# A four-layer graph network on one core: later hand-offs between engines in layers L2 and L3, and a node's own row loaded from the table

## The chip, the core and the metric

The kernel runs on one core of a Trainium2 chip. The metric is the device time of one execution in microseconds (us); the time of a kernel is the median over its runs. The core's engines run side by side, each taking its own instructions in order: PE (TensorE, matrix products), DVE (VectorE, elementwise), ACT (ScalarE, functions and copies), POOL (GpSimd, which here issues the indirect gathers) and SP (SyncE, which issues plain transfers). They wait for each other on semaphores.

## The reference, cut to what matters

There are 6250 nodes with 256 features and 100000 edges sorted by destination node. Four layers follow each other; each takes `h = relu(layernorm(x))` and adds its result to `x`. The change touches the last two:

```python
# L2: attention over a node's incoming edges
h = x @ Wn.T + bn
e = edge_attr @ We.T + be
a = leaky_relu(sum((h[src] + e) * attn, axis=-1), 0.01)
a = exp(a - m[dst]);  a = a / (segment_sum(a, dst)[dst] + 1e-16)
x = x + relu(segment_sum(h[src] * a, dst))
# L3: graph convolution with a self loop
norm = dinv[src] * dinv[dst]           # dinv = 1/sqrt(degree + 1)
x = x + relu(segment_sum((x' @ W)[src] * norm, dst) + b)   # x' = relu(layernorm(x)), src and dst with loops
```

So for each edge a row of a table of nodes has to be fetched by the number in `src`, weighted, and summed at the number in `dst`.

## The kernel before

Nodes are cut into 49 blocks of 128 (`NB`), edges into 98 groups (`G`) of 8 x 128 (`J` = 8 columns of `P` = 128 edges). One layer writes the table that the next one gathers from: L1 writes `xt2` (258 numbers a row) by blocks, L2 gathers from it and writes `xt3` (256 numbers a row), L3 gathers from that and writes the output. A gather (line 130, an indirect DMA that POOL issues) fetches 128 rows by 128 indices, so a group takes 8 of them and a layer 784. All of a layer's gathers depend on the whole table before them.

What is done for a group `g`: DVE makes a one-hot matrix `oh` for each of the 8 columns (line 1095 in L2, with the edge's weight `ex` in it, which ACT makes by an exponential on line 1092; line 1150 in L3, from the destination alone). PE multiplies it with the gathered rows `vg` and sums the 8 products in PSUM (`sum_tiles`, line 681; an f32 product shows as two instructions, so a group is 16). ACT copies the sum to SBUF (`ws`, line 691 in L2, 1175 in L3). Consecutive groups cover overlapping windows of 128 nodes, 64 apart, so when all groups of a block are summed, `sum_block` (line 699) puts three or four windows together with shift matrices on PE: 6 or 8 instructions. `blocks_done(g)` names the block whose last group is `g`: every second group ends one block, and the last group, 97, ends block 48 (block 47 ends with group 96).

What is done for a finished block in L2: `out2` divides by the sum of weights, applies relu (ACT, line 1106), adds to `x`, and makes the layer norm: statistics on DVE (145, 146), a square root on ACT (126), `xn` on DVE (1110). Then `turned2` transposes on PE (1116) with a relu on ACT (1118), and `table3_row` multiplies with `L3_gnn_W` on PE (1124), scales on ACT (1125) into `rows3`, a part of the large tile `big`, and SP writes the block of `xt3` (1126). In L3, `end3` adds the node's own row from `rows3`, scales, adds the bias, applies relu and adds `x` (DVE, 1156, 1157, 1159), and SP writes the output (1161).

The order of the work in both layers is written out by hand under `manual_schedule`: each engine gets its instructions in the order in which the program's loop over `g` names them. In step `g` of L2 the order is: gathers of group `g`; `sum_block` of the block that ended with `g-1`; `turned2` of the one that ended with `g-2`; `one_hot2(g)`; `out2` of the `g-1` block; the group's sum and its copy; `table3_row` of the `g-2` block. In L3: gathers of `g`; `sum_block` of the `g-1` block; the sum of `g`; `one_hot3(g+1)`; the copy; `end3` of the `g-1` block.

Gathered rows lie in 5 buffers in L2 (4 groups are issued before the check `bound2`, whose result decides a branch on line 1078 that is not taken with these inputs) and in 6 buffers in L3. A gather waits until its buffer is free.

Of the kernel before, what the change touches and what calls it, by code (L numbers as in the profile page):

```python
# [10 lines left out]
F32 = mybir.dt.float32  # L11
I32 = mybir.dt.int32
AF = mybir.ActivationFunctionType
OP = mybir.AluOpType
# [3 lines left out]
P = 128  # L18
J = 8
W = 128  # L20
D = 256
# [14 lines left out]
def tile_gnn(ctx: ExitStack, tc: tile.TileContext, a: dict, out: bass.AP, N: int):  # L36
# [287 lines left out]
    def make_windows(ps, pool, win, relw=None):  # L324
# [7 lines left out]
        for i, op in enumerate((OP.min, OP.max)):  # L332
            nc.vector.tensor_reduce(lohi[:, i, :], dstf, AX.X, op)
            t = ps("A", [P, P])
            nc.tensor.transpose(t[:G, :], lohi[:, i, :], ident)
            nc.vector.tensor_reduce(ends[:, i:i + 1], t[:G, :], AX.X, op)
            t = ps("B", [P, P])
            nc.tensor.transpose(t[:, :G], ends[:, i:i + 1].to_broadcast([G, P]), ident[:G, :G])
            nc.vector.tensor_copy(ends_b[:, i, :], t[:, :G])
# [316 lines left out]
    def fast():  # L656
# [406 lines left out]
        ps = fctx.enter_context(Psum("ps2", S=2, A=1, T=2, B=2, C=1))  # L1063
        w3 = weights(wp, "L3_gnn_W", D, D)
        brow = on_all(wp, "L3_gnn_b", D)
        bufs2, ahead = 5, 4
        with tc.tile_pool(name="e2", bufs=2) as ep:
            vgs, gots, sums, normed = {}, {}, {}, {}

            def rows2(g):  # L1070
                vgs[g] = ep.tile([P, J, TR], F32, name="vg", bufs=bufs2)
                gots[g] = [gather(vgs[g][:, j, :], xt2, src_i[:, g * J:(g + 1) * J], j) for j in range(J)]
# [11 lines left out]
            def one_hot2(g):  # L1084

                gs = slice(g * J, (g + 1) * J)
                al = ep.tile([P, J], F32, name="al")
                nc.vector.tensor_tensor(al[:, :, None], vgs[g][:, :, D:D + 1], te[:, gs][:, :, None], OP.add)  # L1088
                leaky(al, al, 0.01)
                nc.vector.tensor_tensor(al, al, shift[:, gs], OP.subtract)  # L1090
                ex = ep.tile([P, J], F32, name="ex")
                nc.scalar.activation(ex, al, AF.Exp)  # L1092
                oh = ep.tile([P, J, P], F32, name="oh")
                for j in range(J):
                    made_g = nc.vector.tensor_scalar(oh[:, j, :], iota, rel[:, g * J + j:g * J + j + 1],  # L1095
                                                     ex[:, j:j + 1], OP.is_equal, OP.mult)
                return oh, made_g

            def out2(b, s):
# [9 lines left out]
                xn = ep.tile([P, D], F32, name="xn", bufs=1)  # L1109
# [3 lines left out]
            def turned2(xn):  # L1113
                t = ps("B", [P, 2, P])
                for k in range(2):
                    nc.tensor.transpose(t[:, k, :], xn[:, k * P:(k + 1) * P], ident)
                hb = ep.tile([P, 2, P], F32, name="hb")
                nc.scalar.activation(hb, t, AF.Relu)
                return hb

            def table3_row(b, hb):
# [3 lines left out]
                nc.scalar.activation(rows3[:, b, :], t, AF.Copy, scale=dinv[:, b:b + 1])  # L1125
                nc.sync.dma_start(xt3[b * P:(b + 1) * P, :], rows3[:, b, :])

            with tc.manual_schedule():
                for g in range(G + 2):
                    if ahead <= g < G:  # L1130
                        rows2(g)
                    summed = [(b, sum_block(sums, b, TR)) for b in blocks_done(g - 1)]
                    turned = [(b, turned2(normed[b])) for b in blocks_done(g - 2)]
                    if g < G:
                        oh, made_g = one_hot2(g)
                    for b, s in summed:
                        normed[b] = out2(b, s)
                    if g < G:
                        sums[g], _ = sum_window(ep, oh, vgs[g], TR, made_g, gots[g])
                    for b, hb in turned:  # L1140
                        table3_row(b, hb)


        with tc.tile_pool(name="e3", bufs=2) as ep, tc.manual_schedule():
            sums = {}

            def one_hot3(g):
                oh = ep.tile([P, J, P], F32, name="oh")
# [3 lines left out]
                return oh, made_g  # L1152

            def end3(b, s):
                r0, r1 = b * P, min(N, (b + 1) * P)
                nc.vector.tensor_tensor(s, s, rows3[:, b, :], OP.add)  # L1156
# [6 lines left out]
            oh, made_g = one_hot3(0)  # L1163
            for g in range(G + 1):
                if g < G:
                    vg = ep.tile([P, J, D], F32, name="vg", bufs=6)
                    got = [gather(vg[:, j, :], xt3, src_i[:, g * J:(g + 1) * J], j) for j in range(J)]
                summed = [(b, sum_block(sums, b, D)) for b in blocks_done(g - 1)]
                if g < G:
                    s = ps("S", [P, D])  # L1170
                    sum_tiles(s, [(oh[:, j, :], vg[:, j, :]) for j in range(J)], made_g, got)
                    if g + 1 < G:
                        oh, made_g = one_hot3(g + 1)
                    sums[g] = ep.tile([P, D], F32, name="ws", bufs=6)
                    nc.scalar.activation(sums[g], s, AF.Copy)
                for b, s in summed:
                    end3(b, s)
# [343 lines left out]
```

## Time and profile before

| | us |
|---|---|
| median of 6 runs | 4505.54 (4501.85 to 4507.66) |
| the profiled execution, device time | 4501.38 |
| its span, first to last instruction | 4499.6 |
| granted TensorE clock, mean share of full speed | 0.823 |

| part of the span | from, us | to, us | what is there |
|---|---|---|---|
| L2, gathers | 2497.8 | 3483.2 | 784 gathers, first start to last end |
| between | 3483.2 | 3502.0 | no gather |
| L3, gathers | 3502.0 | 4484.8 | 784 gathers |
| end | 4484.8 | 4499.6 | no gather |

Layers L0 and L1 and the part between L1 and L2 take the first 2497.8 us; the program that the change touches runs after them. Times of lines are from the span's start. A line of a timeline reads: start, duration, engine, line, operation, output and inputs with shapes, how many instructions are merged, and in brackets how long the engine was idle before and what ended the wait. The L-numbers of lines (L130) are lines of the kernel, not layers.

### The profile page before, as it was taken

The page shows a single profiled execution, that of the slowest core. Times are in us where ns is not written, and L with a number is a line of the kernel's source. Part 1 is how long each engine was busy: PE and PEld are TensorE (multiplying, and loading weights), DVE is VectorE, ACT ScalarE, POOL GpSimd, SP SyncE. Part 2 cuts the span into 40 slices and gives each one's busy share as a digit, 9 for nine tenths or more (in the row PEclk, how much of TensorE's full clock was granted, in tenths as well). Part 3 has the DMA queues.
Part 4 walks back from the last instruction along what each step waited for, and adds up shares of the span by engine and source line. Part 5 has one row for each costly group of instructions (what it writes and reads, how often), then busy time and mean ns, then how long its engine had stood idle before and what let it go on. Part 6 is the DMA issues. An engine that isn't in the chain of part 4 may idle for free. (4 is left out here: it accounts for less than half of the span.)

```text
span 4499.6 us, 42030 instructions
## 1 busy us (share of the span) xinstructions
PE 3068.7 (68%) x12132; PEld 2381.2 (53%) x12133; DVE 2101.7 (47%) x6391; ACT 619.7 (14%) x1559; POOL 3057.8 (68%) x3215
## 2 busy tenths in 40 slices
PE   7788888888897666666556566666566556666656
PEld 4377777776645444444445345445455444444444
DVE  5476655665524566766667333333333222222222
ACT  3211010000124100000000122222222000000000
POOL 0377777777501677777777677777777677777776
PEclk9888888888898777777887688888888788788888
DMA  3355555555500344444444344444443333333333
GB/s 105 113 180 168 162 159 161 161 163 161 155 1 14 110 128 125 123 125 123 129 126 115 88 112 113 111 113 113 112 113 110 97 112 111 112 112 111 112 112 101
DMA packets 258740, 536.78 MB, mean 119 GB/s; under 512 B 65096, under 2 KB 144966, under 8 KB 258502
## 3 DMA queue, kind: packets, MB, share of 16 engines
q0 software_dynamic: 137984, 364.28, 28.5%
q1 hardware_dynamic: 107750, 156.85, 11.3%
q10 hardware_dynamic: 12768, 12.85, 0.9%
q8 instruction: 105, 1.72, 0.2%
q14 instruction: 133, 1.09, 0.1%
HBM read 504.57 MB, written 29.15 MB: 119 GB/s over the span
## 5 line engine op out<-in xcount | busy, mean ns | idle before, releaser
L130 POOL DMA_INDIRECT vg<-xt,src_i x1568 | 1488.4, 949 | 519.1 <-issue 486.4
L681 PE MATMUL ps_S<-vg,oh 128*128 128x258 f32 (+1 forms) x3136 | 992.0, 485 | 775.6 <-DMA vg<-xt,src_i 409.2
L681 PEld LDWEIGHTS ps_S<-vg,oh 128*128 128x128 f32 x3136 | 765.1, 250 | 994.3 <-issue 386.8
L130 POOL DMA_INDIRECT xbuf<-vt,src_i x784 | 783.0, 999 | 241.1 <-issue 211.0
L130 POOL DMA_INDIRECT big<-ht,src_i x784 | 743.5, 948 | 246.3 <-issue 181.1
L681 PE MATMUL ps_S<-oh,big 128*128 128x128 f32 x1568 | 310.6, 379 | 338.1 <-DVE big L1026 296.5
L1150 DVE TENSOR_SCALAR oh<-iota,rel 128x128 f32<-128x128 f32 x784 | 166.8, 302 | 740.9 <-PE ps_S L681 738.7
L681 PE MATMUL ps_S<-xbuf,oh 128*128 128x265 f32 x1568 | 487.1, 476 | 12.9 <-issue 11.6
L681 PEld LDWEIGHTS ps_S<-oh,big 128*128 128x128 f32 x1568 | 288.4, 284 | 368.6 <-DVE big L1026 247.5
L681 PEld LDWEIGHTS ps_S<-xbuf,oh 128*128 128x128 f32 x1568 | 368.0, 241 | 99.2 <-issue 16.3
L763 PE MATMUL ps_A<-scw,to 128*128 128x16 f32 x1568 | 224.3, 287 | 114.5 <-DVE to L748 114.5
L763 PEld LDWEIGHTS ps_A<-scw,to 128*128 128x128 f32 x1568 | 220.7, 224 | 133.8 <-issue 85.6
L1095 DVE TENSOR_SCALAR oh<-iota,rel,ex 128x128 f32<-128x128 f32 x784 | 214.5, 369 | 145.6 <-ACT ex L1092 145.6
L699 PE MATMUL ps_T<-ws,shifts 128*128 128x265 f32 (+2 forms) x1164 | 278.7, 382 | 0.0
L691 ACT ACTIVATE ws<-ps_S 128x265 f32<-128x265 f32 (+1 forms) x196 | 76.3, 389 | 1226.1 <-PE ps_S L681 1226.1
L1026 DVE TENSOR_TENSOR big<-big,ps_A 128x384 f32<-128x384 f32 (+1 forms) x294 | 132.3, 505 | 230.4 <-DMA big<-ht,src_i 225.6
L699 PEld LDWEIGHTS ps_T<-ws,shifts 128*128 128x128 f32 x1164 | 220.8, 190 | 33.7
L836 DVE TENSOR_TENSOR xbuf<-xbuf,ps_E 128x2048 f32<-128x2048 f32 x98 | 223.6, 2282 | 21.5 <-ACT ps_E L774 21.5
L980 PE MATMUL ps_A<-wr,rb 99*128 99x384 f32 (+1 forms) x588 | 214.0, 504 | 9.4 <-DMA rb<-in_rbf 9.4
L1088 DVE TENSOR_TENSOR al<-vg,te 128x8 f32<-128x8 f32 x98 | 16.4, 168 | 426.1 <-DMA vg<-xt,src_i 426.1
L988 DVE TENSOR_SCALAR oh<-iota,rel,cut 128x128 f32<-128x128 f32 x784 | 211.3, 361 | 0.0
L900 POOL TENSOR_TENSOR xbuf<-xbuf,bout 128x1024 f32<-128x1024 f32 (+1 forms) x13 | 29.0, 2228 | 256.5 <-ACT xn L898 249.6
(226 smaller groups left out, 3043.7 us busy)
## 6 DMA issues: line engine op xcount, KB each, us to landing
drow<-in_dst_row SPq DMA_DIRECT2D x98, 512.0 KB
ea<-in_edge_attr SPq DMA_DIRECT2D x98, 512.0 KB
vg<-xt,src_i POOLq DMA_INDIRECT x1568
xbuf<-vt,src_i POOLq DMA_INDIRECT x784
big<-ht,src_i POOLq DMA_INDIRECT x784
rb<-in_rbf SPq DMA_DIRECT2D x196, 49.5 KB
vt<-row SPq DMA_DIRECT2D x49, 132.5 KB
xt<-row SPq DMA_DIRECT2D x49, 129.0 KB
```

What stands on the lines that cost most here:

```text
L130: return nc.gpsimd.indirect_dma_start(out=rows, out_offset=None, in_=table, in_offset=bass.IndirectOffsetOnAxis(ap=idx[:, j:j + 1], axis=0))
L681: m = wait_for(nc.tensor.matmul(s, l, r, start=j == 0, stop=j == len(pairs) - 1), made)
L691: nc.scalar.activation(ws, s, AF.Copy)
L699: nc.tensor.matmul(t, shift_by(s), sums[g], start=i == 0, stop=i == len(parts) - 1)
L763: nc.tensor.matmul(dgs[g][:, j, :], tos[g][:, j * P:(j + 1) * P], scw[:, g // 2, g % 2, :], start=True, stop=True)
L836: made_g = nc.vector.tensor_tensor(vals, vals, ex[:, :, :, None].to_broadcast([P, J, H, HD]), OP.mult)
L900: nc.gpsimd.tensor_tensor(x[:, b0:b1, :], x[:, b0:b1, :], w1["bout"][:, None, :].to_broadcast([P, b1 - b0, D]), OP.add)
L980: filtered[g] = nc.tensor.matmul(t, rbs[g][0:33 * n, g % 2, q, :], wr3[0:33 * n, 0:n, :], start=True, stop=True)
L988: nc.vector.tensor_scalar(ohs[g][:, j, :], iota, rel[:, c], w1["cut"][:, c], OP.is_equal, OP.mult)
L1026: made_g = nc.vector.tensor_tensor(hg[:, js, :], hg[:, js, :], t, OP.mult)
L1095: made_g = nc.vector.tensor_scalar(oh[:, j, :], iota, rel[:, g * J + j:g * J + j + 1], ex[:, j:j + 1], OP.is_equal, OP.mult)
L1150: made_g = nc.vector.tensor_scalar(oh[:, j, :], iota, rel[:, g * J + j:g * J + j + 1], None, OP.is_equal)
```

## The change

In L2 and L3, whatever one engine makes for another is used at least one step of a group later than it is made, as written in the loop:

- L2: `one_hot2(g+1)` is made in step `g` (before, `one_hot2(g)`). The sum's copy (`taken`) is made one step after the sum. `sum_block` comes at 2 steps after the block's last group, `out2` at 3, `turned2` at 4, its relu `hb` at 5, `table3_row` at 6, the scaled row and its write (`row3`) at 7. Before they came at 1, 1, 2, 2, 2 and 2. The loop has 105 steps where it had 100.
- L2: gathered rows lie in six views of `big`, used in the order 3, 4, 5, 0, 1, 2; a gather waits by hand for the end of the sum that used the view six groups earlier. Three groups are gathered before the check, where it was four. PSUM has three slots for sums (it had two), and the tag `A` is gone.
- L3: one-hots are made two steps ahead, the copy is made one step after the sum, `sum_block` comes 2 steps and `end3` 3 steps after the block's last group (before: 1 and 1). PSUM is given out anew: four slots for sums, three for blocks. Rows lie in six views of `big`.
- As `big` now holds gathered rows, `rows3` is gone from both layers: L2 puts a scaled row into one of three small tiles and writes it to `xt3`, and L3 loads a block's own 128 rows back from `xt3` by one SP transfer (`own`) at the step of the block's last group.
- In `make_windows`, which runs only behind branches that are not taken with these inputs, a PSUM tag is `B` where it was `A` (left out below).

```diff
@@ -1060,16 +1060,24 @@
 
 
 
-        ps = fctx.enter_context(Psum("ps2", S=2, A=1, T=2, B=2, C=1))
+
+        psc2 = fctx.enter_context(ExitStack())
+        ps = psc2.enter_context(Psum("ps2", S=3, T=2, B=2, C=1))
         w3 = weights(wp, "L3_gnn_W", D, D)
         brow = on_all(wp, "L3_gnn_b", D)
-        bufs2, ahead = 5, 4
+
+        ahead = 3
         with tc.tile_pool(name="e2", bufs=2) as ep:
-            vgs, gots, sums, normed = {}, {}, {}, {}
+            vgs, gots, ohs, wins, ends, sums, blocks, normed = {}, {}, {}, {}, {}, {}, {}, {}
+            views = []
+            views += [big[:, i * J * TR:(i + 1) * J * TR].rearrange("p (j t) -> p j t", j=J) for i in (3, 4, 5, 0, 1, 2)]
 
             def rows2(g):
-                vgs[g] = ep.tile([P, J, TR], F32, name="vg", bufs=bufs2)
-                gots[g] = [gather(vgs[g][:, j, :], xt2, src_i[:, g * J:(g + 1) * J], j) for j in range(J)]
+                i = g % len(views)
+                vgs[g] = views[i]
+                gots[g] = [wait_for(gather(vgs[g][:, j, :], xt2, src_i[:, g * J:(g + 1) * J], j),
+                                    *([ends[g - len(views)]] if g >= len(views) else []))
+                           for j in range(J)]
 
             with tc.manual_schedule():
                 for g in range(ahead):
@@ -1083,6 +1091,8 @@
 
             def one_hot2(g):
 
+                if g >= G:
+                    return
                 gs = slice(g * J, (g + 1) * J)
                 al = ep.tile([P, J], F32, name="al")
                 nc.vector.tensor_tensor(al[:, :, None], vgs[g][:, :, D:D + 1], te[:, gs][:, :, None], OP.add)
@@ -1090,11 +1100,25 @@
                 nc.vector.tensor_tensor(al, al, shift[:, gs], OP.subtract)
                 ex = ep.tile([P, J], F32, name="ex")
                 nc.scalar.activation(ex, al, AF.Exp)
-                oh = ep.tile([P, J, P], F32, name="oh")
+                oh = ep.tile([P, J, P], F32, name="oh", bufs=4)
                 for j in range(J):
                     made_g = nc.vector.tensor_scalar(oh[:, j, :], iota, rel[:, g * J + j:g * J + j + 1],
                                                      ex[:, j:j + 1], OP.is_equal, OP.mult)
-                return oh, made_g
+                ohs[g] = oh, made_g
+
+            def summed(g, n):
+
+                if g < G:
+                    wins[g] = ps("S", [P, n])
+                    oh, made_g = ohs.pop(g)
+                    ends[g] = sum_tiles(wins[g], [(oh[:, j, :], vgs[g][:, j, :]) for j in range(J)],
+                                        made_g, gots[g])
+
+            def taken(ep, g, n):
+
+                if 0 <= g < G:
+                    sums[g] = ep.tile([P, n], F32, name="ws", bufs=8)
+                    nc.scalar.activation(sums[g], wins.pop(g), AF.Copy)
 
             def out2(b, s):
 
@@ -1106,7 +1130,7 @@
                 nc.scalar.activation(s[:, 0:D], s[:, 0:D], AF.Relu, scale=rd)
                 nc.vector.tensor_tensor(x[:, b, :], x[:, b, :], s[:, 0:D], OP.add)
                 norm_stats(b, b + 1)
-                xn = ep.tile([P, D], F32, name="xn", bufs=1)
+                xn = ep.tile([P, D], F32, name="xn", bufs=2)
                 nc.vector.tensor_scalar(xn, x[:, b, :], mv[:, b, 0:1], rstd[:, b, :], OP.subtract, OP.mult)
                 return xn
 
@@ -1114,67 +1138,90 @@
                 t = ps("B", [P, 2, P])
                 for k in range(2):
                     nc.tensor.transpose(t[:, k, :], xn[:, k * P:(k + 1) * P], ident)
-                hb = ep.tile([P, 2, P], F32, name="hb")
-                nc.scalar.activation(hb, t, AF.Relu)
-                return hb
+                return t
 
             def table3_row(b, hb):
                 t = ps("C", [P, D])
                 for k in range(2):
                     nc.tensor.matmul(t, hb[:, k, :], w3[:, k, :], start=k == 0, stop=k == 1)
-                nc.scalar.activation(rows3[:, b, :], t, AF.Copy, scale=dinv[:, b:b + 1])
-                nc.sync.dma_start(xt3[b * P:(b + 1) * P, :], rows3[:, b, :])
-
+                return t
+
+            def row3(b, t):
+                row = ep.tile([P, D], F32, name="row3", bufs=3)
+                nc.scalar.activation(row, t, AF.Copy, scale=dinv[:, b:b + 1])
+                nc.sync.dma_start(xt3[b * P:(b + 1) * P, :], row)
+
+            turns, hbs, cs = {}, {}, {}
             with tc.manual_schedule():
-                for g in range(G + 2):
-                    if ahead <= g < G:
-                        rows2(g)
-                    summed = [(b, sum_block(sums, b, TR)) for b in blocks_done(g - 1)]
-                    turned = [(b, turned2(normed[b])) for b in blocks_done(g - 2)]
-                    if g < G:
-                        oh, made_g = one_hot2(g)
-                    for b, s in summed:
-                        normed[b] = out2(b, s)
-                    if g < G:
-                        sums[g], _ = sum_window(ep, oh, vgs[g], TR, made_g, gots[g])
-                    for b, hb in turned:
-                        table3_row(b, hb)
-
-
+                one_hot2(0)
+                for g in range(G + 7):
+                    if ahead <= g + 1 < G:
+                        rows2(g + 1)
+                    for b in blocks_done(g - 2):
+                        blocks[b] = sum_block(sums, b, TR)
+                    for b in blocks_done(g - 4):
+                        turns[b] = turned2(normed.pop(b))
+                    for b in blocks_done(g - 6):
+                        cs[b] = table3_row(b, hbs.pop(b))
+                    one_hot2(g + 1)
+                    for b in blocks_done(g - 3):
+                        normed[b] = out2(b, blocks.pop(b))
+                    summed(g, TR)
+                    taken(ep, g - 1, TR)
+                    for b in blocks_done(g - 5):
+                        hbs[b] = ep.tile([P, 2, P], F32, name="hb")
+                        nc.scalar.activation(hbs[b], turns.pop(b), AF.Relu)
+                    for b in blocks_done(g - 7):
+                        row3(b, cs.pop(b))
+
+
+        psc2.close()
+        ps = fctx.enter_context(Psum("ps3", S=4, T=3))
         with tc.tile_pool(name="e3", bufs=2) as ep, tc.manual_schedule():
-            sums = {}
+            sums, blocks, ohs, wins, vgs, gots, ends, owns = {}, {}, {}, {}, {}, {}, {}, {}
+            views = []
+            views += [big[:, i * J * D:(i + 1) * J * D].rearrange("p (j t) -> p j t", j=J)
+                      for i in range(2 * NACC // (J * D))]
 
             def one_hot3(g):
-                oh = ep.tile([P, J, P], F32, name="oh")
+                if g >= G:
+                    return
+                oh = ep.tile([P, J, P], F32, name="oh", bufs=4)
                 for j in range(J):
                     made_g = nc.vector.tensor_scalar(oh[:, j, :], iota, rel[:, g * J + j:g * J + j + 1], None,
                                                      OP.is_equal)
-                return oh, made_g
+                ohs[g] = oh, made_g
+
+            def rows3_(g):
+                if g < G:
+                    vgs[g] = views[g % len(views)]
+                    gots[g] = [wait_for(gather(vgs[g][:, j, :], xt3, src_i[:, g * J:(g + 1) * J], j),
+                                        *([ends[g - len(views)]] if g >= len(views) else []))
+                               for j in range(J)]
 
             def end3(b, s):
                 r0, r1 = b * P, min(N, (b + 1) * P)
-                nc.vector.tensor_tensor(s, s, rows3[:, b, :], OP.add)
+                nc.vector.tensor_tensor(s, s, owns[b], OP.add)
                 nc.vector.scalar_tensor_tensor(s, s, dinv[:, b:b + 1], brow, op0=OP.mult, op1=OP.add)
                 y = ep.tile([P, D], F32, name="y3")
                 nc.vector.scalar_tensor_tensor(y, s, 0.0, x[:, b, :], op0=OP.max, op1=OP.add)
                 if r1 > r0:
                     nc.sync.dma_start(out[r0:r1, :], y[0:r1 - r0, :])
 
-            oh, made_g = one_hot3(0)
-            for g in range(G + 1):
-                if g < G:
-                    vg = ep.tile([P, J, D], F32, name="vg", bufs=6)
-                    got = [gather(vg[:, j, :], xt3, src_i[:, g * J:(g + 1) * J], j) for j in range(J)]
-                summed = [(b, sum_block(sums, b, D)) for b in blocks_done(g - 1)]
-                if g < G:
-                    s = ps("S", [P, D])
-                    sum_tiles(s, [(oh[:, j, :], vg[:, j, :]) for j in range(J)], made_g, got)
-                    if g + 1 < G:
-                        oh, made_g = one_hot3(g + 1)
-                    sums[g] = ep.tile([P, D], F32, name="ws", bufs=6)
-                    nc.scalar.activation(sums[g], s, AF.Copy)
-                for b, s in summed:
-                    end3(b, s)
+            one_hot3(0)
+            one_hot3(1)
+            for g in range(G + 3):
+                rows3_(g)
+                for b in blocks_done(g):
+                    owns[b] = ep.tile([P, D], F32, name="own", bufs=3)
+                    nc.sync.dma_start(owns[b], xt3[b * P:(b + 1) * P, :])
+                for b in blocks_done(g - 2):
+                    blocks[b] = sum_block(sums, b, D)
+                summed(g, D)
+                one_hot3(g + 2)
+                taken(ep, g - 1, D)
+                for b in blocks_done(g - 3):
+                    end3(b, blocks.pop(b))
 
 
     def slow():
```

More of the change, by code (lines that the diff above doesn't have):

```diff
@@ L333, in make_windows @@
             nc.vector.tensor_reduce(lohi[:, i, :], dstf, AX.X, op)
-            t = ps("A", [P, P])
+            t = ps("B", [P, P])
             nc.tensor.transpose(t[:G, :], lohi[:, i, :], ident)
```

## The prediction

> **What bounds the kernel now.** I read the busy time by stage first, then the waits of POOL, then the two stretches in which POOL is idle, line by line. Busy time in five stretches (us; columns PE, PEld, DVE, ACT, POOL, then the granted TensorE clock):
>
> ```profile
> 2497.80:3483.20 985.40, 608.23 (x2202) 485.30 (x2202) 350.09 (x1406) 243.44 (x475) 744.07 (x784) 0.83 0.40 112
> 3483.20:3502.00 18.80, 12.14 (x54) 9.21 (x52) 9.47 (x41) 5.61 (x13) 0.00 (x0) 0.94 0.10 30
> 3502.00:4484.80 982.80, 589.27 (x1934) 464.96 (x1934) 226.23 (x910) 37.16 (x97) 744.30 (x784) 0.80 0.38 111
> 4484.80:4499.60 14.80, 5.27 (x24) 4.08 (x22) 2.70 (x6) 0.38 (x1) 0.02 (x1) 0.89 0.10 31
> ```
>
> L2 and L3 each take 784 gathers. POOL is busy 744 of some 984 us, but its gaps are not waits. Its waits from 2497 us on (total us, times, longest):
>
> ```profile
> POOL vg L130 <- issue: 486.4, 1531, 20.4
> POOL vg L130 <- DMA xt<-big: 18.9, 1, 18.9
> POOL vg L130 <- DMA vg<-xt,src_i: 3.7, 3, 3.1
> ```
>
> 1531 gaps wait for nothing that the profile shows: they are 0.30 us each, one behind every gather, except for the 20.4 us before L2's first. Gather (0.95) and gap (0.30) make a start-to-start time of 1.25 us, and 783 x 1.25 = 979 us of L2's 984.4 and L3's 981.9 us from first to last start. What is left over is 3.1 us at one gather in L2 (the thirty-third, behind the branch on line 1078), and some 2.4 and 2.7 us by which gathers beside DVE's work are longer than 0.95 (1.01 to 1.04 us beside the one-hots of 4002, 4010 and 4021 us). So POOL's issue rate sets both layers, and apart from it there are only the two stretches without gathers, in which a chain runs: the last gather lands, the rest of the layer is made, and its result is written.
>
> **The steady part: what the change can gain there.** PE waits 349.6 us for `oh` of line 1095 and DVE 738.7 us for PE's sums before line 1150; these are waits of engines with room, and the later hand-offs may remove all of them without starting one gather earlier. What could be gained is the 3.1 us and the 5.1 us of longer gathers. The first stays: at the branch POOL waits for the landing of the gather before it (2536.64 to 2540.67), now the 24th and not the 32nd; the flag it tests was made at 2500.3 and DVE passed the branch at 2510.4, long before 24 x 1.25 = 30 us have passed since 2497.8. The second stays too, as the same one-hots are made at the same pace; its ends are 0 and twice the 5.1 us.
>
> The Trainium skill, "Perfetto Trace Analysis", section "Optimization Strategies", says to keep the matmul engine as busy as one can and to speed up whatever it waits for. By it the 349.6 us that PE waits for one-hots would be the size of the gain, a time near 4156 us. This trace disagrees: 1531 gaps of POOL wait for no engine at all.
>
> Does a new wait reach POOL? A view comes free at the end of the sum six groups before. In groups of 10.02 us, group g-6 starts 60 us ahead of group g; it takes 10 us to issue, 2 to land, up to 10 for the step that the sum now lies behind and up to 6.7 for the sum. That leaves over 30 us: no cost, and three views fewer would be needed before POOL stops. `own` (49 transfers of 128 KB on SP) is issued with its block's last group, 30 us before `end3`; a write of that size took 2.6 us from its scaled row to the next gather (3499.35 to 3502.01): no cost (uncovered, it would be 2.6 us once, at the end), and SP's later output write stands behind it by one issue of 0.33 us. Dropping `rows3` costs ACT and SP the same instructions as before.
>
> **The first drain, L2 to L3.** Now (start, duration, idle before):
>
> ```profile
> 3485.59 0.17 DVE L1090 TENSOR_TENSOR al<-al,shift 128x8 f32<-128x8 f32 x1
> 3486.03 0.20 ACT L1092 ACTIVATE ex<-al 128x8 f32<-128x8 f32 x1
> 3486.27 2.14 DVE L1095 TENSOR_SCALAR oh<-iota,rel,ex 128x128 f32<-128x128 f32 x8 [0.51 <-ACT ex L1092]
> 3488.46 3.75 PE L681 MATMUL ps_S<-vg,oh 128*128 128x258 f32 x16 [1.10 <-DVE oh L1095]
> 3493.56 0.16 DVE L1104 TENSOR_SCALAR rd<-ps_T 128x1 f32<-128x1 f32 x1 [2.09 <-PE ps_T L699]
> 3498.88 0.47 ACT L1125 ACTIVATE big<-ps_C,dinv 128x256 f32<-128x256 f32 x1 [1.22 <-PE ps_C L1124]
> ```
>
> When the last gather lands (3485.2), block 47 has already been summed (1.90 us, at 3485.46); its `out2` runs beside the last sum, and only block 48 follows. By the new lags block 46 is at `out2`, block 47 not yet summed, and the order on each engine is fixed. Three things come into the chain:
> - An exponential behind a square root needs a table load. Before, `ex` of group 97 followed that of 96 with no square root between; now `out2` of block 45 lies between `ex` of 96 and of 97. Such a load is seen at 3475.76: 1.28 us, begun when `al` was there, with `ex` right behind. By those rows `oh` would start at 3487.37, 1.10 later. The sum ends at 3493.31.
> - PE sums block 47 next: 1.90 us by the row of 3485.46, so DVE starts its `out2` at about 3495.1.
> - `out2` of 47, from `rd` to the end of `xn`, is a chain between DVE and ACT that took 3.12 us for block 48 (3493.56 to 3496.68). Block 48's can begin only behind it on DVE: 3498.2, where it began at 3493.56. Its own sum is done by then.
>
> That is 4.7 us; behind it the chain is the one of before. With the free-running overlap between engines and `table3_row` of 47 ahead of 48's (1.0 us, partly beside the transposes' relu) my bounds are 4.0 and 5.5. Rows of blocks 46, 47 and 48 are written within 3 us, where it was two: 0 to 0.5, I take 0.2.
>
> The Trainium skill, "ScalarE: Activation LUTs", section "What ACT_TABLE_LOAD costs", adds a drain of about 1.38 us to a load of 1.28. By it the whole change would cost 1.4 us more. In this trace `ex` starts 0.02 us behind the load (3477.06), so I leave the drain out.
>
> **The second drain, the end.** PE now, from the last two groups on:
>
> ```profile
> 4476.77 6.58 PE L681 MATMUL ps_S<-vg,oh 128*128 128x256 f32 x16 [6.35 <-DMA vg<-xt,src_i]
> 4483.19 1.89 PE L699 MATMUL ps_T<-ws,shifts 128*128 128x256 f32 x8
> 4486.99 3.69 PE L681 MATMUL ps_S<-vg,oh 128*128 128x256 f32 x16 [1.91 <-DMA vg<-xt,src_i]
> 4490.52 1.46 PE L699 MATMUL ps_T<-ws,shifts 128*128 128x256 f32 x6
> ```
>
> Two things change. First, block 47's sum, which ran at 4483.19 while group 97 was landing, falls behind the last sum, and its `end3` (4492.01 to 4493.44, so 1.43) ahead of block 48's: 1.89 + 2 x 1.43 less what 48 had to wait anyway (4490.68 to 4493.44, 2.76) is 2.0 us. Second, the last sum loses what kept the clock up. Group 96's sum, after 6.35 us idle, had a granted clock of 0.54 and took 6.58; group 97's, after 1.91 us idle, had 1.00 and took 3.69. In L3 the even groups' sums took 5.2 to 6.7 us, with a median of 6.0. With `sum_block` now a step later it follows the odd groups' sums, not the even ones', and the last group finds PE idle since some 5 us. I take 6.0, so 2.3 us more; ends 0 (it stays at 3.69) and 3.0. Sum of the second drain: 4.3 us. In the first drain the last sum follows group 96's closely, so it stays at full clock.
>
> **The sum.** 4.7 + 0.2 + 2.0 + 2.3 = 9.2 us. On the profiled execution's 4501.38 that is 4510.6; the median of before lies 4.2 above that execution, so against it I predict 4514.7, +0.20%. The line between no change and slower is 0.2%, 9.0 us, about what a measurement of this kernel can tell from no change; the forecast lies just over it.
>
> **The rivals.**
> - The other side, not slower: the last L3 sum stays warm. It decides alone: from 0.2 us less than my 6.0 us on, the total is under 9.0 us; at 3.69 it is 6.9 us, 4512.4. For it: odd sums of 3.69 exist, and 5 us idle is less than the 6.35 of the slow ones. Against it: early in L3 odd sums after about 5 us idle took 5.2. Chance 0.31.
> - The change doesn't do what it says at the tails: engines don't keep the loop's order. For it: `al` of group 0 ran at 2509.82, ahead of DVE's branch that stands before it. If block 47 is summed ahead of the last sum in both layers, 1.9 + 3.1 and 2.0 go: 2.2 us, 4507.7. Chance 0.10.
> - Contention: one-hots made earlier fall beside other gathers. If every group of L3 had one gather of 1.03 and not 0.95, 98 x 0.08 = 7.8 us: 17.0 us, 4522.5. Against it: one-hots still start when a sum frees their slot. Chance 0.10.
> - Faster: the drains cost nothing and both the 3.1 and 5.1 us go: 4497.3, which isn't even 0.2%. Chance 0.04, for what I don't see.
>
> **How the numbers follow.** The forecast, 9.0 to about 13 us, has 0.45; with contention slower has 0.55. The warm sum and the kept order make 0.41 for no change. The range: drains at 4.0 + 0 + 2.0 + 0 less 3 of the 5.1 us is 3.0; drains at 5.5 + 0.5 + 2.0 + 3.0 and 4 us of the contention is 15: 4508.5 to 4520.5. By its own bounds alone the likeliest case has 4514.6 to 4518.5.
>
> **What would show it.** Right: the start-to-start time of gathers stays at 1.25 us in both layers; PE's and DVE's waits shrink; the gap without gathers between L2 and L3 grows from 18.9 to about 23.7 us, with a table load before the last `ex`, and line 699 for block 47 behind the last sum in both layers; the end from the last gather grows from 14.8 to about 19.1. Wrong: gathers that wait for PE, DVE or an earlier landing more than once, or a gap between layers no longer than before.

## The result, and the profile after

The changed kernel takes 4514.08 us (median of 17 runs, 4509.93 to 4518.18) where the kernel before takes 4502.94 (37 runs, the six shown at first among them). The ratio is 1.0025 with a 95% interval of 1.0018 to 1.0031, so 8 to 14 us slower. Predicted were 4514.7 and slower; the time lies in the range. That the change costs time is clear; the line of 0.2% that the prediction drew lies within the interval, so on which side of that line the loss falls is not decided. The reasons were right in kind and place. But of the four terms of the sum, the first drain and the slow last sum were too small, the rest of the end was too large, and the third write of a row did not show; and two costs in L2, an instruction of POOL's at the branch and longer gathers, were not in the sum at all.

In seven of the twelve experiments every kernel, the one before too, had a median of 5210 to 5260 us, and in their traces PE starts its instructions slowly; these seven stand last, each beside the kernel before on the same chip.

Busy time by stage of the profiled execution (span 4513.9 us, 14.3 over before; columns as before: PE, PEld, DVE, ACT, POOL, granted clock):

```profile
2474.20:2495.40 21.20, 11.59 (x36) 7.04 (x35) 12.10 (x32) 1.98 (x8) 0.95 (x1) 0.61 0.08 23
2495.40:3485.00 989.60, 612.07 (x2184) 482.16 (x2184) 349.00 (x1399) 226.74 (x465) 746.26 (x784) 0.81 0.40 111
3485.00:3511.90 26.90, 18.81 (x71) 14.15 (x69) 8.91 (x36) 9.18 (x21) 0.06 (x2) 0.82 0.10 32
3511.90:4494.90 983.00, 590.80 (x1926) 465.04 (x1926) 229.04 (x923) 37.16 (x97) 744.49 (x784) 0.79 0.40 118
4494.90:4513.90 19.00, 9.76 (x30) 7.77 (x30) 2.60 (x6) 0.38 (x1) 0.00 (x0) 0.68 0.08 24
```

Of the 14.3 us, L2's gathers take 4.2 (985.4 to 989.6), the stretch between the layers 8.0 (POOL's idle time, 18.86 to 26.84; the rows are cut at tenths), L3's gathers 0.2, the end 4.2 (14.8 to 19.0); the time up to L2's first gather is 2.3 shorter, in a part that the change leaves alone. POOL's waits (total us, times, longest):

```profile
POOL big L130 <- issue: 458.7, 1506, 0.3
POOL big L130 <- DMA xt<-row: 26.8, 1, 26.8
POOL big L130 <- DVE oh L1105: 5.1, 1, 5.1
```

As before, almost every gap is the 0.30 us that waits for nothing. Gathers still start every 1.25 us: no new wait reached POOL in the steady part. What grew is the wait for the table's last rows and the one gap behind the branch, which was 3.1 us (the 5.1 us that the profile puts down to DVE's one-hot). In L2 the gathers themselves grew too, from 949 to 952 ns on average.

The chain in the first drain, from the last landing on (start, duration, idle before):

```profile
3487.49 0.17 DVE L1100 TENSOR_TENSOR al<-al,shift 128x8 f32<-128x8 f32 x1
3487.74 1.28 ACT L1102 ACT_TABLE_LOAD   x1 [4.38 <-DVE al L1100]
3489.28 2.14 DVE L1105 TENSOR_SCALAR oh<-iota,rel,ex 128x128 f32<-128x128 f32 x8 [1.62 <-ACT ex L1102]
3491.47 5.44 PE L681 MATMUL ps_S<-big,oh 128*128 128x258 f32 x16 [1.85 <-DVE oh L1105]
3496.75 1.90 PE L699 MATMUL ps_T<-ws,shifts 128*128 128x258 f32 x8
3498.69 0.16 DVE L1128 TENSOR_SCALAR rd<-ps_T 128x1 f32<-128x1 f32 x1 [4.21 <-PE ps_T L699]
3501.61 0.15 DVE L1128 TENSOR_SCALAR rd<-ps_T 128x1 f32<-128x1 f32 x1
3506.59 2.08 PE L1146 MATMUL ps_C<-l_gnn_w,hb 128*128 128x256 f32 x4 [0.56 <-ACT row L1151]
3508.76 0.47 ACT L1151 ACTIVATE row<-ps_C,dinv 128x256 f32<-128x256 f32 x1 [2.22 <-PE ps_C L1146]
```

Everything that the prediction put into this chain is there: the table load, block 47's sum behind the last group's, its `out2` (3498.69) ahead of block 48's (3501.61). Two things are there that it didn't have: the last sum takes 5.44 us where it took 3.75, and block 48's product waits 0.56 us for the scaling of block 47's row and then takes 2.08 us where it took 1.13. That product ran at half the clock, and so did nearly all of the last sum of L3 (granted clock third from the end):

```profile
4497.00:4503.60 6.60, 6.60 (x17) 5.29 (x18) 0.00 (x0) 0.00 (x0) 0.00 (x0) 0.53 0.00 0
3506.60:3508.70 2.10, 2.07 (x4) 1.17 (x4) 0.00 (x0) 0.00 (x0) 0.00 (x0) 0.50 0.18 62
```

PE at the end:

```profile
4486.92 3.69 PE L681 MATMUL ps_S<-big,oh 128*128 128x256 f32 x16 [1.75 <-DMA big<-xt,src_i]
4497.00 6.74 PE L681 MATMUL ps_S<-big,oh 128*128 128x256 f32 x16 [6.39 <-DMA big<-xt,src_i]
4503.57 3.18 PE L699 MATMUL ps_T<-ws,shifts 128*128 128x256 f32 x14
```

The parity has turned round, as said: group 96's sum is now the fast one, the last group's is slow after 6.39 us idle, and both blocks' sums (14 instructions) stand behind it.

### The profile page after: what moved, and what is told of

Same layout as the page of the kernel before. It is cut to its first block, busy times and chain, and to the rows that moved or that the text cites. A ratio compares the mean times of both kernels' runs of the same rounds, so it can differ in the third digit from the quotient of the medians.

```text
span 4513.9 us, 42171 instructions
## 1 busy us (share of the span) xinstructions
PE 3083.2 (68%) x12132; PEld 2388.7 (53%) x12133; DVE 2103.5 (47%) x6391; ACT 606.0 (13%) x1557; POOL 3059.4 (68%) x3215
## 3 DMA queue, kind: packets, MB, share of 16 engines
q14 instruction: 135, 1.11, 0.1%
## 5 line engine op out<-in xcount | busy, mean ns | idle before, releaser
L130 POOL DMA_INDIRECT big<-xt,src_i x1568 | 1490.8, 951 | 528.9 <-issue 458.7
L681 PE MATMUL ps_S<-big,oh 128*128 128x258 f32 (+1 forms) x3136 | 934.2, 463 | 501.3 <-DMA big<-xt,src_i 408.2
L681 PEld LDWEIGHTS ps_S<-big,oh 128*128 128x128 f32 x3136 | 737.5, 240 | 702.4 <-issue 389.9
L1191 DVE TENSOR_SCALAR oh<-iota,rel 128x128 f32<-128x128 f32 x784 | 166.9, 302 | 728.3 <-PE ps_S L681 721.6
L699 PE MATMUL ps_T<-ws,shifts 128*128 128x265 f32 (+2 forms) x1164 | 314.5, 408 | 274.3 <-ACT ws L1121 274.3
L1098 DVE TENSOR_TENSOR al<-big,te 128x8 f32<-128x8 f32 x98 | 16.4, 168 | 484.7 <-DMA big<-xt,src_i 484.7
L1121 ACT ACTIVATE ws<-ps_S 128x258 f32<-128x258 f32 (+1 forms) x196 | 73.5, 375 | 959.6 <-PE ps_S L681 959.6
```

Of the source, the lines that this page charges most:

```text
L130: return nc.gpsimd.indirect_dma_start(out=rows, out_offset=None, in_=table, in_offset=bass.IndirectOffsetOnAxis(ap=idx[:, j:j + 1], axis=0))
L681: m = wait_for(nc.tensor.matmul(s, l, r, start=j == 0, stop=j == len(pairs) - 1), made)
L699: nc.tensor.matmul(t, shift_by(s), sums[g], start=i == 0, stop=i == len(parts) - 1)
L1121: nc.scalar.activation(sums[g], wins.pop(g), AF.Copy)
```

## The experiments

Two theories. D: the loss lies in the two drains, where the later hand-offs put one block's work behind the last sum and let PE's clock drop. S: it lies in the steady part, in what the lags, the gathers into `big` or the own rows cost all the time.

**Lags put back, the rest of the change kept.** The edit, in L2 and in the same way in L3:

```diff
-                for g in range(G + 7):
+                for g in range(G + 2):
...
-                    for b in blocks_done(g - 2):
+                    for b in blocks_done(g - 1):
                         blocks[b] = sum_block(sums, b, TR)
...
-                    one_hot2(g + 1)
-                    for b in blocks_done(g - 3):
+                    one_hot2(g)
+                    for b in blocks_done(g - 1):
                         normed[b] = out2(b, blocks.pop(b))
                     summed(g, TR)
-                    taken(ep, g - 1, TR)
+                    if g < G:
+                        taken(ep, g, TR)
```

> Both layers' lags put back to those of before; of the change are left the six views in big, three groups ahead, the small row tiles, the own rows loaded from the table, and PSUM's slots. Theory D (the loss lies in the two drains): gap between L2 and L3 19 +- 1 us (26.8 as changed), end 14.8 +- 1 (19.0 as changed), gathers at 1.253 to 1.258 us on average; total that of before plus at most 2 us, ratio 1.0000 to 1.0006. Rival S (the steady part: gathers into big, longer gathers beside DVE, own rows): gathers over 1.26 us on average in L2 or L3, ratio 1.002 or more.

Measured: 4503.04 us against 4500.83 for the kernel before on the same chip, ratio 1.0004 (0.9995 to 1.0013). By stage:

```profile
2494.20:3481.50 987.30, 604.36 (x2201) 483.26 (x2202) 349.92 (x1406) 243.52 (x475) 743.90 (x784) 0.83 0.42 111
3481.50:3500.30 18.80, 12.15 (x54) 9.25 (x52) 7.03 (x29) 5.61 (x13) 0.04 (x1) 0.94 0.09 30
4484.10:4498.50 14.40, 4.99 (x22) 4.08 (x22) 2.54 (x6) 0.38 (x1) 0.00 (x0) 0.87 0.11 32
```

The gap is 18.8 us and the end 14.5 (the row is cut at tenths), nearly as in the kernel before (18.9 and 14.8); so the lags make the loss of 8.0 and 4.2 us, and the views, the row tiles and the own rows cost nothing in either. Theory D held. L2 is 1.9 us longer than before, and that is the branch alone (5.2 us for 3.1). With the lags L2 had been 2.3 us longer still: its gathers took 952 ns on average with them and 949 without. That small part goes to theory S, in L2 only: the traces of the four kernels with L2's later hand-offs that were not slowed by PE have 28 to 37 gathers over 1 us in L2, the three without have 11 to 18. L3's gathers took 983.8 us here, 982.8 before and 983.0 as changed.

**The product's slot, and PE kept warm.** Two edits at different ends:

```diff
-        ps = psc2.enter_context(Psum("ps2", S=3, T=2, B=2, C=1))
+        ps = psc2.enter_context(Psum("ps2", S=2, T=2, B=2, C=2))
...
                 summed(g, D)
+                if g == G - 2:
+                    t = ps("S", [P, D])
+                    for i in range(12):
+                        nc.tensor.matmul(t, shift_by(0), sums[g - 2], start=i == 0, stop=i == 11)
                 one_hot3(g + 2)
```

> The changed kernel with two edits at different ends. L2: two PSUM slots for table3_row and two for sums (one and three as changed). L3: 12 products of stored values behind group 96's sum, into a slot that nothing reads, so that PE is idle for less before the last sum. Theory D: block 48's product no longer waits for the scaling of block 47's row, gap 26.8 less 0.6 to 1.0; the last sum of L3 takes 3.7 us and not 6.7, the end falls from 19.0 to about 16.0. If the slot had no part in it, the gap stays; if the last sum is slow for another reason than PE's idle time, the end stays at 19.0.

Measured: 4511.55 us in one run (4500.83 for the kernel before), gap 25.3 us, end 16.1. PE at the end, and the two products of line 1146 at the end of the first drain:

```profile
4485.74 3.69 PE L681 MATMUL ps_S<-big,oh 128*128 128x256 f32 x16 [2.23 <-DMA big<-xt,src_i]
4489.26 5.34 PE L1224 MATMUL ps_S<-ws,shifts 128*128 128x256 f32 x24
4495.90 3.69 PE L681 MATMUL ps_S<-big,oh 128*128 128x256 f32 x16 [1.29 <-DMA big<-xt,src_i]
3506.29 1.89 PE L1146 MATMUL ps_C<-l_gnn_w,hb 128*128 128x256 f32 x8
```

With 5.34 us of work for nothing in front of it, the same last sum takes 3.69 us and not 6.74, and the end falls by 3.0 (19.03 to 16.06). The granted clock in that sum is 1.00, where it was 0.53. So the slow sum is one of clock, and 3.0 of the end's 4.2 us are that. In the other gap, the two products ran back to back, eight instructions in 1.89 us; 1.5 us are gone, more than the 0.6 to 1.0 expected: 0.56 of waiting, and 0.95 by which the product had been slow. It now ran at a granted clock of 1.00; whether the wait had brought the drop is not shown.

**One more block behind the last sum.** Every lag of a block's work raised by two steps, in both layers (and four buffers for own rows where there were three); the first of them:

```diff
-                    for b in blocks_done(g - 2):
+                    for b in blocks_done(g - 4):
                         blocks[b] = sum_block(sums, b, TR)
```

> The changed kernel with every lag of a block's work raised by two more steps in both layers, so that one more block (46) stands behind the last group's sum. Theory D: L2's gap grows by out2 of one more block, 3.1 us, and in part its sum of 1.9, to 30 to 32 us; the end by 1.9 + 0 to 1.4, to 21 to 22.5; total 5 to 9 us over the changed kernel. Rival (the loss has nothing to do with how many blocks wait behind the last sum): gap and end stay at 26.8 and 19.0.

Measured: 4516.48 us, ratio 1.0035 (1.0022 to 1.0048); gap 28.4, end 19.4. By the medians this is not clear of the changed kernel (1.0018 to 1.0031), and the profiled execution was 13 us above its own median, spread over all layers, so only its gap and its end are read. Both are below what was expected, as the total is (4.5 us over the changed kernel by the ratios), because in this execution the last sums took 3.75 and 5.38 us where the changed kernel's took 5.44 and 6.74. Without the sums, the gap is 24.7 against 21.4, 3.3 us more for one more `out2`, and the end 14.0 against 12.3, 1.7 us more for one more block sum. The steps are of the size that theory D gives; the expectation had missed that the sum's own time can differ from kernel to kernel.

**The old order at the tails only.** Lags as changed in all of the steady part, the old order from group 96 on:

> The changed kernel with its lags in all of the steady part, and the order of before only at the two tails: from group 96 on in L2, and for blocks 47 and 48 in L3, block 47 is summed and finished ahead of the last group's sum. Theory D: as good as old_lags_third but for the table load ahead of the last exponential, which stays: gap 20 +- 1 us, end 14.8 +- 1, ratio to before 1.000 to 1.001. Rival S: lags in the steady part cost or gain something of their own, so that L2 or L3 from first to last gather differs by over 3 us from old_lags_third.

Measured: 4518.10 us, ratio 1.0037 (1.0024 to 1.0051), a miss. The gap was not 20 but 31.6 us, 2.3 of it by a last sum of 6.00 us. My written-out tail put the rows of blocks 44 and 45 and the relu of block 46 ahead of the last exponential on ACT, and `out2` of block 46 ahead of the last one-hot on DVE. Block 46's relu waited for its transposes, which stood behind block 47's sum on PE, and the last group waited for all of it:

```profile
3499.46 0.17 DVE L1100 TENSOR_TENSOR al<-al,shift 128x8 f32<-128x8 f32 x1
3506.14 2.14 DVE L1105 TENSOR_SCALAR oh<-iota,rel,ex 128x128 f32<-128x128 f32 x8 [6.52 <-ACT ex L1102]
```

So work in front of the last group's own costs time as work behind it does, as far as it doesn't fit into the wait for the landing. The end, where block 47 alone was put in front, was 16.4 us with a last sum of 5.38; without the sums that is 11.0, and 11.1 in the kernel before. It is the kernel before's end but for the clock. For rival S: L2 from first to last gather took 992.0 us here, 4.7 over old_lags_third; 2.4 of that is a gather that was 3 ns longer in this execution in all layers (a median of 949 ns for 946), and the other 2.3 are as much as in the changed kernel.

**Three groups ahead in the kernel before.** `bufs2, ahead = 5, 3` for `5, 4`:

> The kernel before with three groups of L2 gathered ahead of the check and not four; nothing else. It asks whether the longer wait at the branch (5.1 us for the changed kernel, 3.1 before) comes with the smaller number. Theory: the wait is the landing of the gather ahead of it plus the branch itself, whatever the number: 3.1 us at the twenty-fifth gather, total within 3 us of before. Rival: with three groups ahead POOL waits longer: 5.1 us there, and the two other idle stretches as before.

Measured: 4504.27 us in one run, 4497.49 for the kernel before in one run beside it. My theory fell: the wait is 5.3 us.

```profile
POOL vg L130 <- DMA vg<-xt,src_i: 5.3, 1, 5.3
```

The gap between the layers was 20.4 us, so not as before: the last product of the drain took 2.07 us where it took 1.13 before, with the order of before. A drain can thus differ by a microsecond with the clock alone. POOL's instruction at the branch, first in the kernel before, then here (line, operation, times, duration in ns):

```profile
L1078 POOLq INC_SWDGE_SEM  x1: 388/388/388, 2539.6 to 2539.6; - x1
```

```profile
L1078 POOLq INC_SWDGE_SEM  x1: 2355/2355/2355, 2530.3 to 2530.3; - x1
```

It took 2.36 us in place of 0.39, and 2.36 in the changed kernel as well. Two us of the change's loss come with three groups in place of four; why the instruction takes longer then is open.

**Where PE issues slowly.** Seven runs, on three chips, were of this kind. In L3 of the first of them:

```profile
4317.95 0.38 PE L681 MATMUL ps_S<-big,oh 128*128 128x256 f32 x1 [1.72 <-issue]
4319.35 0.38 PE L681 MATMUL ps_S<-big,oh 128*128 128x256 f32 x1 [1.02 <-issue]
4320.75 0.59 PE L681 MATMUL ps_S<-big,oh 128*128 128x256 f32 x1 [1.03 <-issue]
```

PE waits for nothing, yet starts an instruction only every 1.4 us for a while. Over that whole run POOL waited 248.3 us in 82 gaps for releases that the profile can't place. Four kernels ran on the first chip, beside 5246.52 us for the kernel before; L2 lags back, L3 lags back, both back, and two slots for the product:

> The changed kernel with L2's lags put back to those of before (one-hot in its own step, copy at once, sum_block and out2 one step after a block's last group, the rest two steps after); views in big, row tiles, own rows and L3 as changed. Theory D (the loss lies in the two drains, where the lags put block 47's work behind the last sum): the gap without gathers between L2 and L3 falls from 26.8 us to 19 +- 1, the end stays at 19.0, the total is some 8 us under the changed kernel, 4506, a ratio to before of 1.0008. Rival S (the loss lies in the steady part: gathers into big, longer gathers beside DVE, loads of own rows): the gap may shrink, but L2 from first to last gather stays 4 us longer and the total stays near 4514.

> The changed kernel with L3's lags put back to those of before (one-hot one step ahead, copy at once, sum_block and end3 one step after a block's last group); own rows are still loaded and L2 is as changed. Theory D: the end behind the last gather falls from 19.0 us to 14.8 +- 1, the last sum of L3 runs at full clock in 3.7 us instead of 6.7, the gap between the layers stays near 26.8; total 4.2 us under the changed kernel, 4510. Rival S: the end shrinks by under 1 us or L3 from first to last gather changes; total near 4514.

> The changed kernel with both layers' lags put back: left of the change are the six views in big, three groups gathered ahead, the small row tiles, the own rows loaded from the table, and PSUM's slots. Theory D: gap 19, end 14.8, total that of before plus at most the 2 us by which the wait at the branch grew: 4503 to 4506, ratio 1.0000 to 1.0006. Rival S: what is left of the change is what costs, ratio 1.002 or more.

> The changed kernel with two PSUM slots for table3_row and two for L2's sums (one and three as changed). Theory D with the slot as one of its terms: block 48's product no longer waits for the scaling of block 47's row (0.56 us in the changed kernel), the gap falls by 0.6 to 1.0 us, to about 26. If the slot had no part in it, the gap stays at 26.8 +- 0.3; the two sums' slots cost nothing in the steady part by either.

Measured: ratios 1.0022 (1.0011 to 1.0034), 0.9983 (0.9972 to 0.9995) and 1.0018 (1.0009 to 1.0027), and one run of 5234.35 us for the last. None of these tests the theories as meant, as gathers now wait for PE. But they order the kernels otherwise: the two that keep L2's later hand-offs (L3's lags back, and two slots for the product) lie below the kernel before, with gaps between the layers of 32.2 and 36.9 us; the two with old lags in L2 lie above it, with 57.8 and 55.4. Between L3's lags back and both back L2's lags are the only difference, and the intervals lie apart: where PE was late, L2's later hand-offs gained, by these ratios some 0.35%. The second chip (before: 5210.36 us) had both lags back again, 1.0028 (1.0017 to 1.0040), gap 55.6, and the slot and warm kernel, one run of 5217.79, gap 41.2:

> The same kernel as both_old_lags (both layers' lags put back, the rest of the change kept), where the kernel before takes some 4503 us and POOL issues without waits. Theory D (the loss lies in the two drains): gap between L2 and L3 19 +- 1 us (26.8 as changed), end 14.8 +- 1 (19.0 as changed), gathers at 1.25 us; total that of before plus at most the 2 us by which the wait at the branch grew, ratio 1.0000 to 1.0006. Rival S (the steady part: gathers into big, longer gathers beside DVE, own rows): gathers over 1.253 us on average in L2 or L3, ratio 1.002 or more.

> The changed kernel with two edits that touch different ends. L2: two PSUM slots for table3_row and two for sums (one and three as changed). L3: 12 products of stored values with a shift matrix are added behind group 96's sum into a PSUM slot that nothing reads, so that PE is idle for less before the last sum. Theory D: block 48's product no longer waits for the scaling of block 47's row, gap 26.8 less 0.6 to 1.0; the last sum of L3 takes 3.7 us and not 6.7, the end falls from 19.0 to about 16.0. If PSUM's slot had no part in it, the gap stays; if the last sum is slow for another reason than PE's idle time, the end stays at 19.0.

Last, a version meant to beat both, the kernel before with a shorter last group in L1, L2 and L3. The core of the edit:

```diff
-                m = wait_for(nc.tensor.matmul(s, l, r, start=j == 0, stop=j == len(pairs) - 1), made)
-                if j == 0:
-                    wait_for(m, *got)
+                m = nc.tensor.matmul(s, l, r, start=j == 0, stop=j == len(pairs) - 1)
+                if made is not None:
+                    wait_for(m, made)
+                    if j == 0:
+                        wait_for(m, *got)
...
+                for lo, hi in ((0, 4), (4, 7), (7, J)) if g == G - 1 else ((0, J),):
```

> The kernel before, with its order, buffers and lags, and only the last group of L1, L2 and L3 treated otherwise. Its sum doesn't wait for all 8 gathers and all one-hots at once: each column's product waits for its own. In L2 the last group's weights and one-hots are made in three parts (columns 0 to 3, 4 to 6, 7), so that only column 7's work follows the last landing. In L1 the reduction of edge features of the last group is done after the last block's layer norm. Theory D (only the stretches without gathers are left to gain from or to lose): gap between L1 and L2 20.4 to about 17.5 us, between L2 and L3 18.9 to about 14 (one-hots 2.14 less 0.27, products 3.75 less 0.47), end 14.8 to about 11.6 (3.69 less 0.46); gathers stay at 1.25 us; total some 11 us under before, ratio 0.9975, below 0.9985 with its whole interval. Rival: these chains are set by something else than the last group's own work (landing of other gathers, DVE's other work), and the total stays within 3 us of before.

On the third chip, PE was slow too: 5240.99 us against 5247.00, ratio 0.9990 (0.9982 to 0.9999). That is faster than before there, by 0.1%, but the gaps it was made for are filled with PE's waits (44.9 us between L2 and L3), so its sum can't be read, and whether it beats the kernel before at 4503 us is open.

## Why the prediction was right, and where its steps were off

- **POOL's rate sets both layers, and the waits of PE and DVE are worth nothing.** Right: PE's wait for L2's `oh` fell from 349.6 to 88.5 us (and a wait of 274.3 us for ACT's copies came up), DVE's for PE's sums in L3 from 738.7 to 721.6, and no gather gained by it; L3's gathers took 983.0 us for 982.8. The Trainium skill, "Perfetto Trace Analysis", section "Optimization Strategies", which the prediction cites, speaks of engines "that are blocking the critical path"; L2's one-hots did not, so the page and this trace don't disagree.
- **"The first stays" (3.1 us at the branch).** Wrong: 5.1. I took the landing for the whole of the wait and left out the instruction behind it, which took 2.36 us for 0.39: 2.0 us, not in the sum.
- **"The second stays" (longer gathers beside DVE).** Right in L3, 2.3 us off in L2.
- **First drain, 4.7 + 0.2.** It was 8.0. The table load moved the one-hot by 1.11 us (1.10 said); block 47's sum and `out2` delayed block 48's by 3.4 (3.6 said). The 0.2 for a third write did not show: from the last scaled row to the next gather 3.10 us, before 3.13. The step that failed is "the last sum follows group 96's closely, so it stays at full clock": it follows by 1.85 us and took 1.7 more. And the slot of `table3_row` was not in the sum: from `xn` to the last row 4.15 us, where it was 2.20, of which 1.5 went with a second slot.
- **Second drain, 2.0 + 2.3.** It was 4.2, near the 4.3 said only because two errors cancel, which is luck: the sum at half clock cost 3.05 (6.74 for 3.69, after 6.39 us idle and not 5), the rest 1.2. Of that rest the chain behind the sum is 1.7 (4.50 for 2.76), and the last write was 0.5 shorter than before.
- **The rivals.** A warm last sum is what slot_and_warm_again made by force, and the end fell by 3.0 where the rival's price was 2.3. That the written order isn't kept did not happen: both block sums stood behind the last sum. (Its price was also off: it takes 1.9 + 3.1 out of a term in which block 47 has 3.6, so by the prediction's own numbers 3.6 us were left and not 2.2.) Longer gathers came in L2, 2.2 us, and not in L3, where the rival had 7.8.

That the predicted time lies 0.6 us from the measured one is luck as well: the prediction added 9.2 us to 4505.54, the median of six runs; the median of 37 is 2.6 lower, and the change cost 11.1.

The sum of 9.2 us stands beside 11.1 between the medians and 14.3 between the two profiled executions. By stage, 4.2 + 8.0 + 0.2 + 4.2 make 16.6 us, of which L0 and L1, which the change leaves alone, gave 2.3 back in the profiled execution. From 9.2 to 16.6 it is 2.0 for the branch, 2.2 for the longer gathers in L2, 3.1 for the first drain and 0.2 for L3's gathers, less 0.1 at the end.

## What to carry to other kernels

When one queue sets the pace of the steady part at a fixed rate, as POOL's gathers do here, more distance between the other engines has nothing to gain there; it is paid in every drain, once for each block of work that it leaves behind the last result. Ask of every lag what stands behind the last arrival, what stands ahead of it on the same engine, and whether PE is still at full clock by then. A change of this kind can be worth its price where the other engines are what is late: the same lags in L2 gained when PE was slow.

## What the runs showed of the hardware that was not expected

PE's clock can drop in the middle of a burst, and an idle stretch of 1.85 us was enough. In the changed kernel's trace the granted clock is 1.00 or 0.50, and every change of it lies on one grid of 3.41 us. Three windows of that grid, to within 0.1 us, around the changed kernel's last sum in L2 (it starts at 3491.47; PE's busy time is the second number, the granted clock the third from the end):

```profile
3486.05:3489.46 3.41, 3.41 (x17) 2.77 (x15) 0.68 (x4) 1.71 (x3) 0.00 (x0) 1.00 0.05 19
3489.46:3492.87 3.41, 1.56 (x7) 1.25 (x7) 2.77 (x12) 1.13 (x3) 0.00 (x0) 0.99 0.00 0
3492.87:3496.29 3.42, 3.42 (x9) 2.68 (x8) 1.03 (x4) 1.86 (x5) 0.00 (x0) 0.51 0.12 41
```

The middle window was 1.56 of 3.41 us busy, and in the next the clock was half. The Trainium skill, "TensorE: Matmul & The Clock Gate", section "What's actually happening", has free-running windows of about 3.4 us and a drop to half rate after at least one idle window. The windows agree; that a window must be idle does not, as this one was nearly half busy. The busy share doesn't settle it either: in old_lags_third a window as little busy, with 2.34 us idle ahead of the last sum of L3, kept the clock, and that sum took 3.69 us:

```profile
4484.40:4487.81 3.41, 1.56 (x7) 1.44 (x8) 0.92 (x2) 0.00 (x0) 0.00 (x0) 1.00 0.27 77
4487.81:4491.23 3.42, 3.42 (x16) 2.64 (x14) 0.00 (x0) 0.38 (x1) 0.00 (x0) 1.00 0.01 2
```

That a sum's time depends on where it falls in the windows would explain why the last sums took 3.7 to 6.7 us from kernel to kernel; it is not shown. There is one trace of each kernel, so how far the 1.7 us of the first drain's last sum come back in every execution is open.

What made PE start its instructions slowly on three chips is not known from these runs.
